# Feed-forward pieces between the taps of a deformable convolution, and rolling row buffers in place of padded images

## The chip, the cores and the metric

The kernel runs on one core of one Trainium2 chip. The metric is the device time of one execution in microseconds (us). The engines are called PE (TensorE), DVE (VectorE), ACT (ScalarE), POOL (GpSimd) and SP (SyncE); "PEld" is the weight load of PE. Each engine works through its own list of instructions in order and waits on semaphores that other engines or finished DMAs raise.

## The reference

The input is `x`, four images of 256 channels on a 64 x 64 grid, in float32. Everything is computed in float32.

```python
x = x + conv(ln_c(x))            # ln_c: layer norm over the channels of a pixel
t = tokens(x)                    # 4096 tokens of 256 channels per image
t = t + ffn(ln_t(t))             # ln_t: layer norm over the channels of a token
```

`conv` is three modulated deformable 3 x 3 convolutions, each followed by a relu. In each, an ordinary 3 x 3 convolution gives 27 numbers per pixel: for each of the 9 taps a row offset, a column offset and a mask. Tap k of a pixel reads the image at its shifted, fractional position (bilinear, zeros outside), times the sigmoid of the mask; the 9 x 256 samples of a pixel are then multiplied by a 2304 x 256 matrix.

`ffn` is a mixture of 8 experts. The softmax of 8 logits ranks the experts of a token, the best two are kept with their probabilities as weights, and each expert is `gelu(z @ W1 + b1) @ W2 + b2` with 512 hidden units.

## The kernel before, in words

A framework builds the program: the code names tiles out of pools with a fixed number of buffers, the framework adds the semaphore waits, and a list scheduler puts each engine's instructions into an order that need not be that of the code.

**Work units.** An image is cut into 8 blocks (`NB`) of 512 pixels, that is 8 rows. A stage is one convolution layer on one image; there are 12, ordered in pairs of images: (layer, image) = (0,0), (0,1), (1,0), (1,1), (2,0), (2,1), then the same for images 2 and 3. For each image the input of a layer lies in two places: as a zero-padded image in SBUF (`xpad`, read by the offset convolution) and as a table in DRAM (`tab`), whose row for a pixel holds 256 values and 256 differences to the pixel one row below, so that two neighbouring table rows (4 KB) are all that one sample needs.

**One block of the convolution** is `main_block`. For each tap k there are four groups of 128 pixels. For each group POOL issues an indirect DMA that gathers 128 x 4 KB from `tab` into `g` (L323, 8 buffers); DVE blends the two rows (L330); ACT scales the left column into `s` (L335); DVE adds the right column (L340); PE transposes `s` in two pieces (L345). ACT copies the transposed samples to `sT` (L352), and four 128 x 128 by 128 x 512 matmuls add them to `acc` (L355; the trace holds two records for each). After the ninth tap ACT applies the relu (L365). In layers 0 and 1 DVE copies the result into `xpad`, and PE, ACT and SP transpose it, copy it and store it in the table of the next layer (L377, L382, and `store_steps` with `dd`, L171, for the differences). In layer 2 the block is added to `x`, transposed and stored as tokens `t` (L374 to L387).

**One block of offsets** is `off_block`: 18 matmuls into `po` (L248), a small matmul into `pm` (L261), a sigmoid, and some 14 small DVE operations that give the gather indices `idx` and the blend factors `cf`. `main_block(i, n)` is followed by `off_block(i + 1, n)`, which belongs to the other image of the pair. **`pre_block`** normalises a block of `x` and writes the first table. It runs for images 0 and 1 ahead of all stages, and for images 2 and 3 beside the main blocks of the two layer-2 stages of the first pair.

**The feed-forward** begins when all 12 stages are done, with pools of its own. Per image: `prologue` loads a block of tokens, normalises it, and computes logits, softmax and ranks; `route` turns the choices into slots, sorted by expert, in tiles of 256 slots (39 tiles, `NF`); `dispatch` scatters the normalised tokens to those slots in `zs` in DRAM, by 64 indirect DMAs of 128 rows of 1 KB from POOL (L603); `expert` (39 times) loads the weights of a tile's expert by two indirect DMAs (L616, skipped inside the DMA if the expert is that of the tile before; one buffer), loads the tile from `zs` by SP, transposes it (`ftp`, L631), multiplies by W1 (`ph`, L642), applies gelu (L651), multiplies by W2 (`py`, L657), adds the bias on DVE (`y`, L665) and stores it in `ys`; `combine` gathers the two results of each token (`gy`, L681, 64 indirect DMAs per image), adds them to the token, transposes and stores. The prologue, route and dispatch of image b + 1 and the combine of image b - 1 are placed between the experts of image b.

Two consecutive scatters write the same DRAM tile `zs`, so each waits until the one before has landed.

## Time and profile before

| | |
|---|---|
| three runs | 8577.3, 8572.57, 8595.02 us (median 8577.3) |
| the profiled execution | 8566.52 us, its span 8564.6 us |
| first and last relu of a main block (L365) | at 314.8 and 6287.3 us of the span |
| busy PE, DVE, ACT, POOL | 6694.2, 5057.5, 3344.6, 4441.2 us |
| matmuls of the taps (L355) | 3353.7 us |
| indirect DMAs: gathers / weights / scatters / result gathers | 3456 / 312 / 256 / 256 |

The span falls into two parts: the convolutions up to about 6290 us, and the feed-forward of four images after it. A block of the convolution lasts from one relu group of L365 to the next. "Busy" of PE counts modelled ends of pipelined matmuls. In a wait, the instruction that waited stands before the arrow and what released it after it.

### The profile page before, as it was taken

The page shows a single profiled execution, that of the slowest core. Times are in us where ns is not written, and L with a number is a line of the kernel's source. Part 1 is how long each engine was busy: PE and PEld are TensorE (multiplying, and loading weights), DVE is VectorE, ACT ScalarE, POOL GpSimd, SP SyncE. Part 2 cuts the span into 40 slices and gives each one's busy share as a digit, 9 for nine tenths or more (in the row PEclk, how much of TensorE's full clock was granted, in tenths as well). Part 3 has the DMA queues.
Part 4 walks back from the last instruction along what each step waited for, and adds up shares of the span by engine and source line. Part 5 has one row for each costly group of instructions (what it writes and reads, how often), then busy time and mean ns, then how long its engine had stood idle before and what let it go on. Part 6 is the DMA issues. An engine that isn't in the chain of part 4 may idle for free.

```text
span 8564.6 us, 91686 instructions
## 1 busy us (share of the span) xinstructions
PE 6694.2 (78%) x26776; PEld 3737.0 (44%) x26776; DVE 5057.5 (59%) x11216; ACT 3344.6 (39%) x6860; POOL 4441.2 (52%) x4289
## 2 busy tenths in 40 slices
PE   7888888888888888888888888777753928658285
PEld 3444434444444444444344444343432827547274
DVE  4677767777677777777677777566662323323122
ACT  3454544444444444444444444344421212112011
POOL 0466556665555566566656656466623243433434
PEclk8999999999999999999999999899966969879697
DMA  5899989999899999999989999999942224333243
GB/s 163 278 329 328 329 314 324 335 321 331 316 321 321 315 324 334 328 326 328 324 309 333 322 333 331 358 331 333 335 146 79 87 99 133 113 102 123 82 128 121
DMA packets 791821, 2246.18 MB, mean 262 GB/s; under 512 B 131976, under 2 KB 245128, under 8 KB 789784
## 3 DMA queue, kind: packets, MB, share of 16 engines
q0 software_dynamic: 567168, 1917.26, 63.2%
q1 hardware_dynamic: 224152, 323.06, 11.4%
q8 instruction: 214, 3.51, 0.2%
q14 instruction: 287, 2.35, 0.1%
HBM read 2154.08 MB, written 232.31 MB: 279 GB/s over the span
## 4 chain that ended last, share of the span: by engine, by line
PE 50%; DMA 12%; DVE 12%; ACT 12%; issue 11%; POOL 2%; ACTq 0%; SPq 0%; POOLq 0%; DVEq 0%
PE acc L355 23%; ACT s L335 7%; PE tp L345 7%; PE po L248 6%; DVE g L330 6%; DMA zs<-z,slots 5%; PE ph L642 5%; PE py L657 4%; ACT sT L352 3%; DMA w<-in_W,wrow 3%; DVE s L340 2%; DMA g<-tab,idx 2%; DMA gy<-ys,slots 1%; PE tpo L377 1%; ACT r L365 1%
## 5 line engine op out<-in xcount | busy, mean ns | idle before, releaser
L323 POOL DMA_INDIRECT g<-tab,idx x3456 | 3628.6, 1050 | 2640.4 <-DVE s L340 1812.5
L355 PE MATMUL acc<-sT,wk 128*128 128x512 f32 x6912 | 3353.7, 630 | 347.3 <-ACT sT L352 345.6
L330 DVE SCALAR_TENSOR_TENSOR g<-g,cf 128x512 f32<-128x512 f32 x3456 | 2518.2, 745 | 94.1 <-DMA g<-tab,idx 93.5
L340 DVE SCALAR_TENSOR_TENSOR s<-g,cf,s 128x256 f32<-128x256 f32 x3456 | 1607.0, 483 | 1552.7 <-ACT s L335 1541.1
L335 ACT ACTIVATE s<-g,cf 128x256 f32<-128x256 f32 x3456 | 1682.1, 511 | 1925.6 <-DVE g L330 1886.6
L355 PEld LDWEIGHTS acc<-sT,wk 128*128 128x128 f32 x6912 | 1301.4, 198 | 2024.4 <-issue 1230.2
L345 PE MATMUL tp<-ident,s 128*128 128x128 f32 x6912 | 1024.5, 280 | 340.3 <-DVE s L340 302.7
L352 ACT COPY sT<-tp 128x512 f32<-128x512 f32 x1728 | 927.2, 590 | 865.0 <-PE tp L345 864.6
L345 PEld LDWEIGHTS tp<-ident,s 128*128 128x128 f32 x6912 | 811.2, 143 | 961.8 <-DVE s L340 453.0
L616 POOL DMA_INDIRECT w<-in_W,wrow x312 | 312.7, 1002 | 843.9 <-ACT hT L651 363.1
L248 PE MATMUL po<-xpad,wo 128*32 128x512 f32 x3456 | 719.4, 629 | 32.7 <-ACT xpad L220 20.8
L651 ACT ACTIVATE hT<-ph,w 128x256 f32<-128x256 f32 x624 | 258.8, 470 | 1143.9 <-PE ph L642 1143.5
L642 PE MATMUL ph<-fzT,w 128*128 128x256 f32 x2496 | 592.3, 392 | 65.7 <-DMA w<-in_W,wrow 65.2
L657 PE MATMUL py<-w,hT 128*128 128x256 f32 x2496 | 588.7, 390 | 54.8 <-DMA w<-in_W,wrow 44.9
L631 PE MATMUL ftp<-ident,zt 128*128 128x128 f32 x624 | 96.7, 283 | 613.7 <-DMA zt<-zs 604.2
L642 PEld LDWEIGHTS ph<-fzT,w 128*128 128x128 f32 x2496 | 481.5, 196 | 157.3 <-DMA w<-in_W,wrow 87.2
L657 PEld LDWEIGHTS py<-w,hT 128*128 128x128 f32 x2496 | 475.7, 196 | 131.5 <-issue 42.9
L603 POOL DMA_INDIRECT zs<-z,slots x256 | 251.6, 983 | 483.1 <-DMA zs<-z,slots 345.4
L665 DVE TENSOR_TENSOR y<-py,w 128x512 f32<-128x512 f32 x156 | 107.6, 690 | 466.4 <-PE py L657 466.4
L635 DVE COPY fzT<-ftp 128x512 f32<-128x512 f32 x156 | 107.3, 689 | 438.4 <-PE ph L642 317.7
L631 PEld LDWEIGHTS ftp<-ident,zt 128*128 128x128 f32 x624 | 76.7, 147 | 628.9 <-DMA zt<-zs 606.6
L681 POOL DMA_INDIRECT gy<-ys,slots x256 | 247.1, 965 | 147.5 <-issue 57.9
(136 smaller groups left out, 3073.2 us busy)
## 6 DMA issues: line engine op xcount, KB each, us to landing
g<-tab,idx POOLq DMA_INDIRECT x3456, 6.1
zt<-zs SPq DMA_DIRECT2D x156, 256.0 KB, 3.1
ys<-y SPq DMA_DIRECT2D x156, 256.0 KB, 2.0
tab<-h SPq DMA_DIRECT2D x128, 256.0 KB, 6.5
tab<-hd SPq DMA_DIRECT2D x128, 256.0 KB, 9.0
zs<-nil SPq DMA_DIRECT2D x12, 1664.0 KB, 25.6
xc_pre<-in_x SPq DMA_DIRECT2D x32, 512.0 KB, 4.5
tab<-h_pre SPq DMA_DIRECT2D x64, 256.0 KB, 3.3
```

What stands on the lines that cost most here:

```text
L248: nc.tensor.matmul(po[g * Q : (g + 1) * Q, :], lhsT=wo[:, k, c, :], rhs=xp[:, c, RPB * n + ky : RPB * n + ky + RPB, kx : kx + W], start=(m ...
L323: nc.gpsimd.indirect_dma_start(out=g, out_offset=None, in_=tb, in_offset=bass.IndirectOffsetOnAxis(ap=idx[:, n, j : j + 1], axis=0),)
L330: nc.vector.scalar_tensor_tensor(v[:, :, 0, :], v[:, :, 1, :], cf[:, n, j, 0:1], v[:, :, 0, :], ALU.mult, ALU.add,)
L335: nc.scalar.activation(s, v[:, 0, 0, :], AF.Copy, scale=cf[:, n, j, 1:2])
L340: nc.vector.scalar_tensor_tensor(ss[u], gs[u][:, 1, 0, :], cf[:, n, j, 2:3], ss[u], ALU.mult, ALU.add)
L345: nc.tensor.transpose(tp[:, c, (t0 + u) * P : (t0 + u + 1) * P], ss[u][:, c * P : (c + 1) * P], ident,)
L352: nc.scalar.copy(sT[:, c, :], tp[:, c, :])
L355: nc.tensor.matmul(acc[:, o, :], lhsT=wk[:, k, c, o * P : (o + 1) * P], rhs=sT[:, c, :], start=(k == 0 and c == 0), stop=(k == K - 1 and c ...
L616: nc.gpsimd.indirect_dma_start(out=w, out_offset=None, in_=ins[src], in_offset=bass.IndirectOffsetOnAxis(ap=st["wrow"][:, f : f + 1], axis=0),
L642: nc.tensor.matmul(ph[:, h, :], lhsT=w1[:, o : o + P], rhs=zT[:, c, :], start=(c == 0), stop=(c == CC - 1),)
L651: nc.scalar.activation(hT[:, h0 + h, :], ph[:, h, :], AF.Gelu, bias=w1[:, k : k + 1])
L657: nc.tensor.matmul(py[:, u, :], lhsT=hT[:, h, u * P : (u + 1) * P], rhs=w2[:, h * C : (h + 1) * C], start=(h == 0), stop=(h == HC - 1),)
```

## The change

The program is rewritten as one class, `Weave`, with one set of pools for the whole run.

- **Order of the stages.** (0,0), (1,0), (0,1), (2,0), (1,1), (0,2), (2,1), (1,2), (0,3), (2,2), (1,3), (2,3), so that an image is finished after stages 3, 6, 9 and 11 (counted from 0). Only image 0 is normalised ahead of the stages; `pre_block` of images 1, 2, 3 runs beside stages 0, 3 and 6, right after each main block.
- **Rolling row buffers.** `xpad` goes. Each block of a layer's output is written into a window of 10 rows (`win`, three buffers, four more ones in the first stage); ACT copies one row from and to the neighbouring window, DVE forms `dd` and a copy `vv`, PE transposes both (16 transposes, as before in number), ACT copies them to `hv`, SP stores whole 2 KB table rows. The offsets of block n - 1 of the same image's next layer are computed when block n is there (`rows_done`).
- **Tokens.** The main block of layer 2 ends with `tokens`: the sum with `x`, the normalisation, logits, softmax and ranks, which were `tpo`, `h` and `prologue`. Both `t` and the normalised `z` go to DRAM.
- **The queue.** When an image's last block is done, its `route`, 32 dispatch pieces of two scatters, 39 experts and 16 combine pieces of four result gathers go into a queue with a weight each. After each tap `pump` adds a rate to a credit and takes pieces whose weight it covers. The rate spreads an image's pieces over 2.9, 2.9 and 1.9 stages for images 0, 1, 2; image 3 has no stage after it, and its pieces come one after the other at the end.
- **Buffers.** `g` has 10 buffers in place of 8, `s` 5 in place of 6; expert weights have two buffers, and are skipped if the tile two before had the same expert; `ph` and `py` have one PSUM buffer each in place of two; all transposes share three PSUM banks in place of two buffers of two banks.
- **Engines.** The feed-forward's copies out of PSUM (`fzT`, `zT`, `o`) go from DVE to ACT; half of the relu goes from ACT to DVE; the sigmoid is written with tanh.

The core of the diff, whose new lines are shown with the functions that they call:

```diff
-    with ExitStack() as conv:
-        convolutions(conv, tc, ins, x, B, dram, t_dram, ident, eps_c)
-    with ExitStack() as ffn:
-        feed_forward(ffn, tc, ins, out_v, B, dram, t_dram, ident, eps_t)
+    Weave(ctx, tc, ins, out).run()
...
+    def rows_done(self, l, b, n, wins):
...
+        if n > 0:
+            nc.scalar.copy(w[:, :, 0, 1 : W + 1], wins[n - 1][:, :, RPB, 1 : W + 1])
+            nc.scalar.copy(wins[n - 1][:, :, RPB + 1, 1 : W + 1], w[:, :, 1, 1 : W + 1])
+        self.store_table(l, b, n, w)
+        if n > 0:
+            self.off_block(l, b, n - 1, wins[n - 1])
+        if n == NB - 1:
+            self.off_block(l, b, n, w)
...
+        for k in range(K):
+            sT = self.smT.tile([P, CC, BLK], F32, tag="sT", name=f"sT_{nm}_{k}")
+            for t0 in range(0, TPB, 2):
+                tp = self.ps.tile([P, CC, 2 * P], F32, tag="tp", name=f"tp_{nm}_{k}_{t0}")
...
+                nc.scalar.copy(sT[:, :, t0 * P : (t0 + 2) * P], tp)
...
+            if n == NB - 1 and i + 1 < len(self.stages):
+                self.load_tap(self.stages[i + 1][0], k, i + 1)
+            self.pump()
...
+        nc.scalar.activation(dst[0], src[0], AF.Relu, bias=bk[:, 0:1])
+        nc.vector.tensor_scalar(dst[1], src[1], bk[:, 1:2], 0.0, ALU.add, ALU.max)
+        if l < NL - 1:
+            self.rows_done(l + 1, b, n, wins)
+        else:
+            self.tokens(b, n, r)
...
+    def tokens(self, b, n, r):
...
+        nc.sync.dma_start(self.t_dram[b][n], tok)
+        normalise(nc, self.small, tok, z, self.eps_t, nm)
+        nc.sync.dma_start(self.z_dram[b][n], z)
...
+        if n == grp.n1 - 1:
+            self.enqueue(grp)
...
+    def dispatch(self, grp, n, t):
+        m = n * TPB + t
+        for i in range(2):
+            self.nc.gpsimd.indirect_dma_start(
+                out=self.zs[grp.i % 2],
+                out_offset=bass.IndirectOffsetOnAxis(ap=grp.slots[:, i, m : m + 1], axis=0),
+                in_=grp.z[:, t, :],
+                in_offset=None,
+            )
...
+    def expert(self, grp, f):
...
+        if f == 0:
+            self.weights(grp, 0)
+        if f + 1 < grp.NF:
+            self.weights(grp, f + 1)
+        w1, w2 = self.w1[f % 2], self.w2[f % 2]
...
+            ph = self.ps1.tile([P, 2, FT], F32, tag="ph", name=f"ph_{nm}_{h0}")
...
+    def enqueue(self, grp):
+
+        nb = grp.n1 - grp.n0
+        q = [(2.0, lambda: self.route(grp)), (20.0, lambda: None)]
+        for n in range(nb):
+            q.append((0.0, lambda n=n: self.dispatch_load(grp, n)))
+            for t in range(TPB):
+                q.append((2.0, lambda n=n, t=t: self.dispatch(grp, n, t)))
+        q.append((15.0, lambda: None))
+        for f in range(grp.NF):
+            q.append((8.0, lambda f=f: self.expert(grp, f)))
+        q.append((15.0, lambda: None))
+        for n in range(nb):
+            q.append((0.0, lambda n=n: self.combine_load(grp, n)))
+            for t0 in range(0, TPB, 2):
+                q.append((4.0, lambda n=n, t0=t0: self.combine(grp, n, t0)))
+        taps = grp.stages * NB * K
+        rate = sum(w for w, _ in q) / taps if taps else 0.0
+        self.queue += [(w, rate, fn) for w, fn in q]
+
+    def pump(self):
+        if not self.queue:
+            self.credit = 0.0
+            return
+        self.credit += self.queue[0][1]
+        while self.queue and self.queue[0][0] <= self.credit:
+            w, _, fn = self.queue.pop(0)
+            self.credit -= w
+            fn()
+
+    def run(self):
+
+        self.stages = [
+            (0, 0), (1, 0), (0, 1), (2, 0), (1, 1), (0, 2),
+            (2, 1), (1, 2), (0, 3), (2, 2), (1, 3), (2, 3),
+        ]
+
+        beside = {0: 1, 3: 2, 6: 3}
+
+        self.groups = [Group(b, 0, NB) for b in range(self.B)]
+        for i, (g, s) in enumerate(zip(self.groups, (2.9, 2.9, 1.9, 0))):
+            g.i, g.stages = i, s
...
+        for i in range(len(self.stages)):
+            wins, pre = {}, {}
+            for n in range(NB):
+                self.main_block(i, n, wins)
+                if i in beside:
+                    self.pre_block(beside[i], n, pre, i == 0)
+        while self.queue:
+            self.queue.pop(0)[2]()
```

## The prediction

> **What bounds the kernel now.** I read the busy table by slices first, then windows of single stretches, then the timeline of one tap. The slices:
>
> ```profile
> PE   7888888888888888888888888777753928658285
> POOL 0466556665555566566656656466623243433434
> PEclk8999999999999999999999999899966969879697
> DMA  5899989999899999999989999999942224333243
> ```
>
> Two parts are to be seen: 28 slices in which PE is 80 to 90% busy and the DMA engines over 90%, and 11 in which neither is. The windows give numbers (a stretch of convolution; the first image's scatters; its experts; a dense part of those):
>
> ```profile
> core 0: us, PE busy (x) PEld busy (x) DVE busy (x) ACT busy (x) POOL busy (x), PEclk, DMA share, GB/s
> 1000.00:6170.00 5170.00, 4363.26 (x16281) 2122.60 (x16280) 3648.97 (x7308) 2471.15 (x5090) 3095.43 (x2946) 0.95 0.92 327
> 6388.00:6566.00 178.00, 0.00 (x0) 0.00 (x0) 25.48 (x100) 2.08 (x7) 65.01 (x66) 0.50 0.22 75
> 6566.00:6900.00 334.00, 308.14 (x1545) 263.85 (x1546) 111.66 (x399) 87.83 (x177) 86.77 (x88) 0.99 0.29 93
> 6600.00:6800.00 200.00, 187.03 (x957) 160.84 (x956) 63.37 (x229) 54.23 (x110) 44.48 (x45) 0.99 0.27 89
> ```
>
> The scatters leave PE idle for 178 us; the experts run PE at 93.5%. The scatters in the timeline:
>
> ```profile
> 6421.35 0.97 POOL L603 DMA_INDIRECT zs<-z,slots  x1 [1.71 <-DMA zs<-z,slots]
> 6424.03 0.97 POOL L603 DMA_INDIRECT zs<-z,slots  x1 [1.70 <-DMA zs<-z,slots]
> ```
>
> Each waits for the one before to land: 2.68 us apart. Inside the convolution, a tap where nothing else is interleaved:
>
> ```profile
> 1196.45 3.70 PE L355 MATMUL acc<-sT,wk 128*128 128x512 f32 x8 [0.73 <-ACT sT L352]
> ...
> 1201.70 0.44 PE L345 MATMUL tp<-ident,s 128*128 128x128 f32 x2 [0.90 <-DVE s L340]
> 1202.87 3.70 PE L355 MATMUL acc<-sT,wk 128*128 128x512 f32 x8 [0.73 <-ACT sT L352]
> ```
>
> A tap takes 6.42 us here, and PE waits in it for DVE's samples and for ACT's copy. PE's own work per tap is (3353.7 + 1024.5) / 864 = 5.07 us, from the rows
>
> ```profile
> L355 PE MATMUL acc<-sT,wk 128*128 128x512 f32 x6912 | 3353.7, 630 | 347.3 <-ACT sT L352 345.6
> L345 PE MATMUL tp<-ident,s 128*128 128x128 f32 x6912 | 1024.5, 280 | 340.3 <-DVE s L340 302.7
> ```
>
> Blocks, from relu to relu (a plain one, then one with a normalised block beside it):
>
> ```profile
> 4428.41 1.26 ACT L365 ACTIVATE r<-acc,bk 128x512 f32<-128x512 f32 x2 [0.78 <-PE acc L355]
> 4489.65 1.26 ACT L365 ACTIVATE r<-acc,bk 128x512 f32<-128x512 f32 x2 [0.78 <-PE acc L355]
> ```
> ```profile
> 2695.91 1.26 ACT L365 ACTIVATE r<-acc,bk 128x512 f32<-128x512 f32 x2 [0.78 <-PE acc L355]
> 2760.33 1.26 ACT L365 ACTIVATE r<-acc,bk 128x512 f32<-128x512 f32 x2 [0.59 <-PE acc L355]
> ```
>
> Over the timeline plain blocks take 60 us, those in the two stages with `pre_block` 67; the one change of stage that waits for a table just written costs 94 - 60 = 34. PE is busy about 54 of the 60. So the convolution is bound by PE plus latency between DVE, ACT and PE; the feed-forward, 2277 us after the last relu, by experts on PE and by scatters and gathers one by one.
>
> **The change part by part.** The sum follows the new order; the old one stands at 6287 us at its last relu.
>
> *Start.* Eight normalised blocks go ahead in place of sixteen. In the opening stretch one starts about every 17.5 us together with its offsets: 140, then 85 for gather landing and the first main block, its end included: 225 at the first relu (before: 314.8; bounds 205 and 250).
>
> *Stage 0*, seven further blocks, with a normalised block and a second set of offsets beside each: 67 plus 18 offset matmuls and the small ones, (719.4 + 98.8) / 96 = 8.5: 75 each, 525 (bounds 67, all hidden, and 90, all in series).
>
> *Two stage changes* need the table just written, (0,0) to (1,0) and (1,3) to (2,3): 68. Other changes of stage keep a stage in between.
>
> *Plain blocks*, 7 stages x 8. The transposes are the same in number; DVE gains the copy `vv` (priced by two `xpad` copies, 0.88) and half the relu (0.69, as a copy of this size out of PSUM) and loses the two copies; the chain relu, row copies, `dd`, `vv` is some 2 us longer, and six offset matmuls (2.5 us) now stand in it. I take 60, 3360 (bounds 58 and 63; the three shared PSUM banks argue for the upper one).
>
> *Token blocks with a normalised block* (stages 3 and 6, 16 blocks). PE's list has the token transposes, then transposes of `z`, then logits, then the normalised block, one behind the other, so PE waits through add 1.2, copies 1.2, four statistics 2.3, square root with its table load 1.6, normalising 1.6, copies 1.2, and about 0.2 per hand-over, with a few blends between: 17 us over today's 67. 84 each, 1344. Below: today's prologue took 98 us for eight blocks, pipelined, 12 each: 79. Above: 96, if rank and softmax, 4 us of DVE, and the second table load also stand in the chain, and more blends fall in it.
>
> *Token blocks alone* (stages 9, 11; 16 blocks). No offsets and no table, but without offsets the last stage has 59.5 today, so that gives nothing; the logits come some 8 us later than today's transposes, minus what DVE blends ahead: 66, 1056 (bounds 60 and 75).
>
> Convolution: 225 + 525 + 68 + 3360 + 1344 + 1056 = 6578.
>
> *Experts of images 0 to 2*, 117. Each has (96.7 + 592.3 + 588.7) / 156 = 8.19 us of PE. Fully in PE's idle 6 us per block (2.65 experts a block) each would cost 5.9; at the PE share of the dense window, (54 + 21.7) / 0.935 = 81 per block, 7.9. The scheduled order has taps' transposes between `ph` and `py`, so ACT's gelu is covered. I take 7.5: 878 (upper bound 9.0, with a wait for the single `ph` buffer).
>
> *Scatters.* They now stand in POOL's list with one or two gathers after each. Three POOL issues take 3 x 1.24 (0.94 and 0.30 idle in the timeline) = 3.7 us; an idle machine lands a scatter in 2.4. I take 3.9 from scatter to scatter: 64 x 3.9 = 250 us of POOL, in which 27 taps of 6.67 (18 for image 2) would have passed: 70 + 70 + 130, a little of it caught up at block ends: 240. Gathers queued behind a waiting scatter are `g` tiles for DVE, and ten buffers cover two and a half taps. Below: 3.4, if the next issue never waits, 145. Above: landing as the median gather in the convolution, 6.1, plus issue, 7.1: 850.
>
> The page "DMA: Bandwidth & Descriptors" of the Trainium skill (Queues, rings and completion order; Latency and other measured facts) speaks against the change here: an engine consumes its ring in order, and access to the DRAM takes 0.2 us on average, 2 at high load. By that a scatter in the convolution lands some 1.8 us later than the 2.4 of the trace, an estimate of about 4.5 between scatters and 115 more in the sum, 8548; no row of the trace has a scatter under load.
>
> *Result gathers.* 64 x 1.24 = 80 us of POOL per image, against a spare 60 - 36 x 1.24 = 15 us per block over three blocks (two for image 2): 35 + 35 + 50 = 120 (below 40, if `combine` finds POOL idle).
>
> *Cover.* Some 18 experts fall into token blocks, where PE idles: they cost 3.5 there, -70.
>
> *Tail, image 3.* Tokens 25, route 10, 64 x 2.68 = 172, landing and loading 6, 39 experts at 9.0 (8.36 by the dense window's 200 us, plus the single `ph`) = 351, combine as today's last, 110: 674 (bounds 640 and 710). Double weight buffers remove the waits of `ph` and `py` for weights (110 us in all today); the gelu wait is late next. The DMA bytes that the second buffer adds, 3 x 8 loads of 128 x (1028 + 1280) x 4 bytes or 28 MB, lie beside PE work, since stretched taps need fewer gathers per us than the 327 GB/s.
>
> Span 6578 + 878 + 240 + 120 - 70 + 674 = 8420, with 2 us around it 8422, against 8566.5 of the profiled execution, which lies 0.13% below the median of 8577.3. On the median's scale: **8433 us**, 1.7% less.
>
> **The rivals.**
> (1) *Scatters land late*, and POOL's list holds up the gathers: slower. For it: 92% DMA share and 6.1 us to land a gather. Against it: only two gathers ahead of each scatter. It costs 192 us per us of period over 3.9, and decides at 3.9 + 144 / 192 = 4.65; at 5.5, 8740.
> (2) *Token chains are longer*: 32 blocks. It decides at 4.5 us more per block; at 96 and 75, 8770. For it: DVE has some 65 us of work in the longer kind (36 x 1.23 for samples, 9 for tokens, 5 for normalising, 4 for offsets, 3 for the table). Against it: blended rows wait ready, so taps after it run at 5.1.
> (3) *The pieces don't hide*: a block's matmuls wait at each piece for DVE and ACT to refill; 11 us per expert gives 8845. The scheduled order, which mixes them finely, speaks against it.
> (4) *PE fills up*: 6734 us of PE work (6694 plus 256 transposes), less 350 in the tail, at 90%: 7090, and 674: about 7780; half way, 8080. For it: PE waits in taps that have DVE time to spare. Against it: scatters and chains give PE nothing to do.
>
> **How the numbers follow.** Forecast 0.42 (8300 to 8540), rival 4 0.12, a shortfall that ends near today 0.06, rival 1 0.20, rival 2 0.14, rival 3 0.06. Faster by over 0.3% (about what a measurement of this kernel can tell from no change): 0.42 + 0.12 = 0.54; within 0.06; slower 0.40. The likeliest case's own range is 8300 to 8540; the range for 8 in 10 takes in half of rival 4 and most of 1 and 2: 8100 to 8860.
>
> **What the profile after would show.** Right: relus 60 us apart in stages 1, 2 and 10, about 80 with experts, 84 in stages 3 and 6; scatters at 3.9; the last relu near 7750, and about 670 after it. Wrong: scatters apart by over 4.65 with DVE waiting for `g`; token blocks over 90; PE waiting for `s` right after each `py`.

## The result, and the profile after

The changed kernel takes 8633.36 us (median of four runs, 8624.77 to 8641.94), the kernel before 8577.05: a ratio of 1.0062, 95% interval 1.0043 to 1.0081. It is slower by 0.6%, inside the range of 8100 to 8860, on the other side of no change than forecast.

Times below are compared within one set of runs measured together, because in some sets the kernel before itself took 8680 to 8703 us, and the changed kernel 8902 where it ran beside it (ratio 1.0249, 1.0202 to 1.0296), with ACT standing still for reasons that the trace doesn't name (last section).

The slices of the page of after (busy tenths in 40 slices of the span of 8640.1 us), to be set against those of before:

```profile
PE   5788888877776899988777799998776698777096
PEclk8999999998888999998888899998888899888597
DMA  5887999987777888876787888887797787768233
```

PE is no longer busy in one long stretch and idle in another. Its row rises and falls with the stages: 9 where experts lie between plain blocks (slices 15 to 17 and 24 to 27), 7 in the stages with tokens (9 to 12, 20 to 22). The first image's scatters pull it down in slice 13. DMA falls to 7 in the token stages too, so a full DMA is not what holds them. Windows of single stretches give the numbers. The columns are the window, its length, then busy time (and instructions) of each engine, the granted clock of PE, the DMA share and GB/s. The windows are the opening gathers and first block, plain blocks, eight blocks with tokens and a normalised block, four blocks with scatters, eight plain blocks with experts, and the last image's scatters:

```profile
core 0: us, PE busy (x) PEld busy (x) DVE busy (x) ACT busy (x) POOL busy (x), PEclk, DMA share, GB/s
160.00:268.00 108.00, 59.49 (x157) 26.52 (x152) 50.87 (x104) 31.12 (x61) 45.66 (x47) 0.78 0.99 396
881.00:1376.00 495.00, 419.75 (x1635) 204.04 (x1634) 355.74 (x731) 238.45 (x504) 304.33 (x288) 0.98 0.92 327
1871.50:2576.60 705.10, 518.69 (x2022) 275.30 (x2022) 466.06 (x1124) 314.01 (x615) 323.59 (x287) 0.84 0.70 253
2576.60:2926.00 349.40, 246.88 (x796) 112.41 (x796) 185.29 (x348) 123.44 (x249) 222.37 (x212) 0.86 0.81 270
3229.50:3844.90 615.40, 569.24 (x2423) 341.30 (x2421) 377.89 (x755) 272.46 (x613) 340.44 (x333) 0.99 0.86 302
7998.50:8220.00 221.50, 11.23 (x45) 9.03 (x46) 16.77 (x58) 6.91 (x11) 66.34 (x68) 0.51 0.22 75
```

Only the stretch with experts between plain blocks does what the change is written for: PE is busy for 569.24 of 615.40 us, 92.5%, nearly as in the dense experts of before (93.5%). In the token stage it is 518.69 of 705.10, 74%, and the clock granted to it is 0.84. In the scatter stretch it is 71%.

Three groups of the page of after (busy time, mean ns, idle time before and what ended it) show what is new among the waits, and a fourth line is the row of before that belongs to the second:

```profile
L467 PE MATMUL acc<-sT,wk 128*128 128x512 f32 x6912 | 3393.7, 635 | 216.8 <-ACT sT L464 212.7
L445 DVE SCALAR_TENSOR_TENSOR g<-g,cf 128x512 f32<-128x512 f32 x3456 | 2546.9, 747 | 1384.1 <-DMA g<-tab,idx 1369.3
L664 POOL DMA_INDIRECT zs<-zl,slots x256 | 266.1, 1040 | 399.9 <-DMA zs<-zl,slots 311.3
```
```profile
L330 DVE SCALAR_TENSOR_TENSOR g<-g,cf 128x512 f32<-128x512 f32 x3456 | 2518.2, 745 | 94.1 <-DMA g<-tab,idx 93.5
```

DVE waits 1369 us for gathers, against 93.5 before. That looks like the reason for the loss; an experiment below takes the weight loads out of POOL's list and finds that they are not what the wait or the time comes from. POOL waits 311 us for scatters to land, 116 of it after the last relu.

**Where the time went.** Block by block, from relu to relu of L486 (a stage is counted from its first relu to the first of the next, so that its last block holds the change of stage):

| | prediction | after |
|---|---|---|
| first relu | 225 | 268.4 |
| stage 0, first seven blocks | 525 | 521.2 |
| the two stage changes that wait for a table | 68 | about 32 (91.9 - 75 and 103.4 - 88) |
| plain blocks without pieces (stages 1, 2) | 60.0 | 61.9 on average; 61.6, the last of a stage 66 |
| token blocks with a normalised block (stage 3) | 84 | 88.1 on average; 84.6 to 88.4, the last 101.7 |
| last relu | 7746 | 7998.5 |
| after it | 674 | 641.6 |

So everything that is missing was lost ahead of the last relu (7998.5 - 7746 = 252 us); the end was 32 us shorter than forecast (642 for 674).

### The profile page after: what moved, and what is told of

It is laid out like the page before. It is cut to its first block, busy times and chain, and to the rows that moved or that the text cites. A ratio compares the mean times of both kernels' runs of the same rounds, so it can differ in the third digit from the quotient of the medians.

```text
span 8640.1 us, 92087 instructions
## 1 busy us (share of the span) xinstructions
PE 6778.1 (78%) x27032; PEld 3829.6 (44%) x27032; DVE 4998.0 (58%) x10768; ACT 3516.7 (41%) x7349; POOL 4492.8 (52%) x4289
## 5 line engine op out<-in xcount | busy, mean ns | idle before, releaser
L467 PE MATMUL acc<-sT,wk 128*128 128x512 f32 x6912 | 3393.7, 635 | 216.8 <-ACT sT L464 212.7
L450 ACT ACTIVATE s<-g,cf 128x256 f32<-128x256 f32 x3456 | 1625.8, 510 | 1878.8 <-DVE g L445 1192.4
L455 DVE SCALAR_TENSOR_TENSOR s<-g,cf,s 128x256 f32<-128x256 f32 x3456 | 1577.2, 481 | 912.7 <-ACT s L450 906.4
L459 PE MATMUL tp<-ident,s 128*128 128x128 f32 x6912 | 1078.3, 284 | 515.9 <-DVE s L455 499.6
L464 ACT COPY sT<-tp 128x512 f32<-128x512 f32 x1728 | 961.0, 585 | 887.4 <-PE tp L459 882.0
L731 PE MATMUL py<-w,hT 128*128 128x256 f32 x2496 | 637.4, 388 | 23.0 <-ACT hT L726 20.2
L319 PE MATMUL po<-win,wo 128*32 128x512 f32 x2304 | 410.7, 611 | 102.2 <-ACT win L255 95.1
L664 POOL DMA_INDIRECT zs<-zl,slots x256 | 266.1, 1040 | 399.9 <-DMA zs<-zl,slots 311.3
L319 PE MATMUL po<-win_pre,wo 128*32 128x512 f32 x1152 | 240.2, 713 | 37.5 <-ACT win_pre L255 18.4
L289 ACT COPY hv<-tpv 128x512 f32<-128x512 f32 x384 | 198.3, 599 | 165.0 <-PE tpv L284 163.3
```

The source lines that it names most:

```text
L319: nc.tensor.matmul(po[g * Q : (g + 1) * Q, :], lhsT=self.wo[l][:, k, c, :], rhs=w[:, c, ky : ky + RPB, kx : kx + W], start=(m < NQ), stop= ...
L450: nc.scalar.activation(s, g[:, 0, 0, :], AF.Copy, scale=cf[:, j, 1:2])
L455: nc.vector.scalar_tensor_tensor(ss[u], gs[u][:, 1, 0, :], cf[:, j, 2:3], ss[u], ALU.mult, ALU.add)
L459: nc.tensor.transpose(tp[:, c, u * P : (u + 1) * P], ss[u][:, c * P : (c + 1) * P], self.ident,)
L464: nc.scalar.copy(sT[:, :, t0 * P : (t0 + 2) * P], tp)
L467: nc.tensor.matmul(acc[:, o, :], lhsT=self.wk[k][:, c, o * P : (o + 1) * P], rhs=sT[:, c, :], start=(k == 0 and c == 0), stop=(k == K - 1 ...
```

## The experiments

**The convolution part and the pieces told apart.** `pump` returns at once, so all pieces come after the last stage; each image's `route` runs when the image is finished.

```diff
-        q = [(2.0, lambda: self.route(grp)), (20.0, lambda: None)]
+        self.route(grp)
+        q = []
...
     def pump(self):
+        return
```

> The changed kernel with every feed-forward piece held back until the last convolution block is done (only the routing of an image is computed when the image is finished). It separates the price of the new convolution part (rolling rows, token chains, start) from the price of the pieces that go between the taps. Theory A (the convolution part without pieces is longer than the old one by its token chains, and the pieces then still gain a lot by going between the taps): plain blocks stay at 61.6 us, blocks with tokens and a normalised block at 86, blocks with tokens alone at about 75 with PE idle for some 20 us of each; the last relu near 6870 us, four feed-forwards of about 610 us behind it, 9330 us in all, so that going between the taps is worth about 700 us. Theory B (the pieces cost as much between the taps as they cost alone, and the convolution part is as short as the old one): token-alone blocks at 62 to 64 us, last relu below 6600, total within 2% of the 8633 us.

It took 9375.49 us, 1.0797 (1.0748 to 1.0847) of the kernel before, but ACT's stalls without a releaser came to 1500 us there, and the changed kernel was not beside it. A second run in another set gave 1.0928 (1.0899 to 1.0956) with the same stalls; a third had the changed kernel beside it:

> The changed kernel as the base of the three beside it. Two kinds of measurement have been seen: one in which the kernel before takes 8577 to 8600 us and ACT has under 200 us of idle time without a named releaser, and one in which it takes 8680 to 8703 and kernels derived from the changed one have 900 to 1500 us of such time. In the first kind the ratio is 1.005 again; in the second, if the disturbance reaches the changed kernel more than the one before, 1.02 to 1.035.

> Every piece held back until the last convolution block is done, once more beside the changed kernel, to subtract like from like. Theory A: undisturbed, the last relu comes near 6870 us, and the pieces between the taps cost about 1120 us in the changed kernel (predicted 1168); disturbed, 7120 to 7220 against 8250 to 8300 in the changed kernel, 1100 as well. So the step that failed is the convolution part, which the prediction had at 6578. Theory B: less than 6700 undisturbed, and the pieces cost over 1300.

The changed kernel took 8901.92 us in this set, the kernel with all pieces at the end 9361.36, 1.0780 (1.0716 to 1.0843) of the kernel before. The last relu in each (ACT's instruction, its duration, its start), first with the pieces at the end, then in the changed kernel of the same set:

```profile
L486 ACT ACTIVATE r<-acc,bk x1: 687/687/687, 7091.1 to 7091.1; 128x512 f32<-128x512 f32 x1
```
```profile
L486 ACT ACTIVATE r<-acc,bk x1: 687/687/687, 8259.2 to 8259.2; 128x512 f32<-128x512 f32 x1
```

The difference is 1168 us. The scheduler had lifted the first image's 64 scatters into stages 3 and 6 of the kernel with the pieces at the end, where the second of these stages is 35 us longer than the first; with that, the pieces of three images cost about 1200 us between the taps. The prediction had 878 + 240 + 120 - 70 = 1168. Taken from the first measurement's 7998.5, this leaves about 6800 us for the convolution part alone. Both runs of the subtraction hold the stalls, at about the same rate (ACT's waits without a releaser up to the last relu add up to 821 us of 8259 and 648 of 7091), so 1200 is somewhat too much. Added up stage by stage in the first measurement, which has few such waits, the pieces cost 1146 us (against 495 for a plain stage, 705 for one with tokens and a normalised block, 72 for a block with tokens alone, 16 for the stage change in stage 10), which leaves 6852. So the convolution part takes 6800 to 6850 us, where the prediction had 6578, and the pieces 1150 to 1200. Theory A holds: the pieces were priced right as a sum, the convolution part was not.

It also shows what going between the taps is worth. At the end the four feed-forwards take 9364.9 - 7091.1 = 2274 us, 568 each, as in the kernel before (2277). Three of them cost 1150 to 1200 between the taps in place of 1700. The changed kernel still loses. Its convolution part is 510 to 560 us longer than the old one (6800 to 6850 against 6287; the new one holds the work of tokens and logits, which stood in the feed-forward before), and its feed-forward only 440 to 490 shorter (the pieces and the 642 at the end, against 2277).

**The chains at block ends.** In a token block, the timeline of PE in the changed kernel (start, duration, instruction, idle time before it and what ended it) shows one stop after another:

```profile
1962.87 1.94 PE L517 MATMUL tp_tok<-ident,r 128*128 128x128 f32 x8 [4.91 <-DVE r L509]
1969.55 1.09 PE L530 MATMUL ztp_tok<-ident,z_tok 128*128 128x128 f32 x4 [4.75 <-DVE z_tok L64]
1971.32 1.88 PE L540 MATMUL lp_tok<-gw,zT_tok 128*128 128x8 f32 x8 [0.68 <-ACT zT_tok L536]
...
1982.34 0.66 PE L404 MATMUL tp_pre<-ident,h_pre 128*128 128x128 f32 x2 [4.70 <-DVE h_pre L64]
```

`late_both` moves two of these chains. The transposes of `z`, logits and ranks of a block are computed after the second tap of the next block, and `pre_block` in two halves after the fourth and sixth tap of the main block, in place of behind it.

```diff
             if n == NB - 1 and i + 1 < len(self.stages):
                 self.load_tap(self.stages[i + 1][0], k, i + 1)
+            if hook and k == KP:
+                hook = hook()
+            if hook and k == KP + 2:
+                hook()
+            if k == KL and self.later:
+                self.later()
+                self.later = None
             self.pump()
...
         nc.sync.dma_start(self.z_dram[b][n], z)
+        self.later = lambda: self.rank(b, n, grp, nm, z, lg)
```

> The changed kernel itself once more, as the base of the three kernels that run beside it. In the four runs before this one engines stood still for reasons that their traces don't name (1000 to 1500 us of ACT's idle time has no releaser, against 95 in the kernel before and 167 in the changed kernel), and the kernel before took 1.2% longer than in the first measurement. If this is the chip, the changed kernel shows it too, and its ratio to the kernel before is up to 1.03; on a chip like the first one it is again 1.004 to 1.008.

> The changed kernel with two chains moved away from the ends of blocks: the transposes of the normalised tokens, the logits and the ranks of a block are computed after the second tap of the next block, and the normalised block of the next image in two halves after the fourth and the sixth tap of the main block in place of behind it. Nothing else changes. Theory A (in the token stages PE stands idle for some 20 us of every block because these chains stand one behind the other in its list): blocks with both go from 86 to about 72 us, blocks with tokens alone from 75 to about 65, the first stage's from 75 to 72: 16 x 14 + 16 x 9 + 8 x 3 = 390 us less than the changed kernel beside it, a ratio to that of 0.955 (0.945 to 0.975). Theory B (these blocks are long by the work of DVE and PE that they hold, the order does not matter): less than 100 us, 0.99 or more.

In this set the changed kernel took 8635.08 us, 1.0047 (1.0031 to 1.0063) of the kernel before, as in the first measurement. `late_both` took 8303.82, 0.9661 (0.9644 to 0.9679) of the kernel before: 331 us, or 3.8%, less than the changed kernel. Blocks of stage 3 take 70 to 76 us in place of 85 to 88. By stage, changed kernel and `late_both`: stage 3 705 and 583, stage 6 780 and 690, stage 9 662 and 617, the first seven blocks of stage 11 651 and 608, stage 0 615 and 581; the other stages agree within 20 us each. The first relu comes 28 us later, since both halves of a `pre_block` now stand inside the first main block. Stage 3 in its window (columns as above), and PE in the same place of a block of it:

```profile
1871.40:2454.40 583.00, 474.08 (x1972) 260.63 (x1972) 447.75 (x1107) 297.10 (x604) 310.57 (x287) 0.92 0.86 305
```
```profile
2022.95 1.94 PE L534 MATMUL tp_tok<-ident,r 128*128 128x128 f32 x8 [5.27 <-DVE r L526]
...
2033.03 0.56 PE L551 MATMUL ztp_tok<-ident,z_tok 128*128 128x128 f32 x3 [1.53 <-DVE z_tok L66]
2033.42 3.60 PE L475 MATMUL acc<-sT,wk 128*128 128x512 f32 x8
```

The wait of 4.75 us ahead of the transposes of `z` is 1.53 here, because taps stand in front of it. Over the stage, PE's groups with the two moved chains (busy time, mean ns, idle time before), first in the changed kernel and then in `late_both`:

```profile
L530 PE MATMUL ztp_tok<-ident,z_tok 128*128 128x128 f32 x64 | 17.4, 428 | 41.9 <-DVE z_tok L64 41.9
L404 PE MATMUL tp_pre<-ident,h_pre 128*128 128x128 f32 x64 | 16.8, 380 | 37.5 <-DVE h_pre L64 32.5 <-DVE w_tok L584 5.0
```
```profile
L551 PE MATMUL ztp_tok<-ident,z_tok 128*128 128x128 f32 x64 | 10.8, 285 | 6.7 <-DVE z_tok L66 6.7
L412 PE MATMUL tp_pre<-ident,h_pre 128*128 128x128 f32 x56 | 9.7, 285 | 3.2 <-ACT sT L472 1.8 <-DVE h_pre L66 1.5
```

Some 70 us of waits are gone; the wait ahead of the tokens' own transposes, which were not moved, stays (46.6 us, then 46.8). PE's busy share of the stage rises from 74 to 81%. Theory A holds with a gain of 331 for 390. This is the largest single cause that an experiment shows: of the 210 us that stage 3 takes over a plain stage (705 against 495), 122 come from the order of two chains, and the other 88 stay with the work itself and the chain that was not moved.

**Scatters that don't wait for each other.** The second choices go to a tensor of their own, which no expert reads.

```diff
-                out=self.zs[grp.i % 2],
+                out=(self.zs, self.zo)[i][grp.i % 2],
```

> The changed kernel in which the scatters of the second choices go to another DRAM tensor than those of the first choices, so that a scatter waits for the landing of the one two before it instead of the one before it. Left out of the computation: the experts see empty slots in place of the second choices; the number and the size of all instructions stay. Theory A (in the scatter blocks the waits of POOL's list for the landing hold up the gathers): the 12 scatter blocks fall from about 88 us to about 75 (36 x 1.24 + 18 x 1.29 = 68 us of issue is what remains on POOL), the 64 scatters after the last block take about 90 us in place of 172, the one block of 150 us also goes back to 90 because the last scatter then stands further ahead of the first expert in the lists: together some 130 + 80 + 55, about 8370 us (8300 to 8450). Theory B (the number of POOL issues, not the wait, stretches these blocks): scatter blocks stay above 84 us and only the part after the last relu gets shorter, 8500 us or more.

It took 8769.48 us, 1.0089 (1.0061 to 1.0116) of the kernel before; `fill_late` and `gap` of the same set stand at 1.0223 and 1.0306. POOL's waits ahead of scatters are 311.3 us in the changed kernel, in 193 waits (row of L664 above). In this one, for the half of the scatters that write `zs` (waits in us, and how many):

```profile
  DMA zs<-zl,slots: 41.4, 40
```

After the last relu 559 us are left in place of 643, as expected (84 us). Inside the stages the gain is small: stage 4 takes 656 us against 681 and 686 in those two, stage 7 647 against 671 and 663. That is some 23 us per image, where 130 were expected for three. Neither theory fits as it stands, and B comes nearer: the waits went, but the scheduler then put up to 22 scatters into a block (32 in one), and 36 gathers and 22 scatters at 1.27 us of POOL each are 74 us, longer than a plain block (these blocks took 80 to 93). So the landing is about a quarter of the hundred us that an image's scatters cost between gathers. That the rest is their place in POOL's list is likely from this count, but no run shows it alone.

**Scatters spread thinner.**

```diff
-                q.append((2.0, lambda n=n, t=t: self.dispatch(grp, n, t)))
+                q.append((5.0, lambda n=n, t=t: self.dispatch(grp, n, t)))
```

> The changed kernel with a weight of 5 in place of 2 for each piece of two scatters, so that about 10 scatters fall into a block over six blocks in place of 18 over three and a half; the experts stand a little closer for it. In the lists the first expert of the third image stands 18 gathers behind its last scatter, in place of 15 ahead. Theory A (POOL has some 15 us to spare per block, and 18 scatters with their waits need 44): scatter blocks go from 88 to 66 to 70 us, the 64 scatters of an image cost 40 us in place of 100, the block of 150 us is gone: 150 to 200 us less than the changed kernel beside it, ratio 0.977 to 0.983. Theory B (each scatter costs what it costs, 1.5 us, wherever it stands): within 0.5% of the changed kernel, but for the 55 us of the one block.

8637.02 us, the changed kernel beside it 8635.08: nothing. Yet the scatter blocks did shrink. Six of them:

```profile
2591.80:3026.70 434.90, 333.10 (x1204) 155.81 (x1204) 269.73 (x529) 184.06 (x374) 291.34 (x276) 0.94 0.86 299
```

That is 72.5 us a block with 10 scatters. Against plain blocks of 61.6 the first image's 64 scatters cost 70 us in place of 99, and the block of 150 us is 85. Stages 4, 7 and 10 together are 183 us shorter. But the seven experts per image that stood in stage 4 or 7 now stand further on: stages 5, 6, 8, 9 and 11 are 174 us longer together. An expert costs 5.5 us where 2.7 of them fall into a plain block, 6.4 where 3.1 do ((654.6 - 495) / 25), and 6 to 10 in the token stages. The total is that of theory B, but for another reason: the scatters did get cheaper, as theory A has it. The pieces of an image have a fixed number of taps to lie in, and what was won at one end of them was lost at the other.

**The block that stood still.** In the changed kernel 150.6 us pass between the third and the fourth relu of stage 10. One row of PE's timeline tells why:

```profile
6834.74 1.09 PE L705 MATMUL ftp<-ident,zt 128*128 128x128 f32 x4 [54.64 <-DMA zt<-zs]
```

The first expert of the third image stands in PE's list ahead of taps whose gathers stand in POOL's list ahead of the last scatters; it needs all scatters, so PE stops until POOL has worked through its list with the buffers it has. `gap` raises the credit between the last scatter and the first expert.

```diff
-        q.append((15.0, lambda: None))
+        q.append((15.0 if grp.i != 2 else 75.0, lambda: None))
         for f in range(grp.NF):
```

> The changed kernel in which, for the third image alone, the credit to be saved between the last scatter and the first expert is 75 in place of 15. In the lists the first expert's transposes then stand behind the last scatter's place by 17 gathers, as for the first two images (18), in place of ahead of it by 15. Theory A (PE waits at that expert for all scatters, while the gathers that the scatters stand behind wait for PE to free their buffers' successors): the third block of the eleventh stage falls from 150 to about 90 us, the experts that start later are pushed into the last stage at about 6 us each, total 8575 to 8600 us. Theory B (that block is long by its 21 scatters and its first experts themselves): it stays above 120 us and the total within 15 us of 8633.

The block takes 85.7 us, so the mechanism is right, as theory A has it, but the total does not gain: 8945.94, 1.0306 (1.0276 to 1.0336) of the kernel before, with `fill_late` at 1.0223 in the same set. From stage 10 to the last relu it takes 769 + 702 us, `fill_late`, which keeps the stall, 773 + 668. The higher weight raises the rate at which the later pieces come (four to five experts a block in place of four), and by these stage times they cost what the stall had cost.

**The zero-filling stores.**

```diff
-        for z in self.zs:
-            r = 0
-            while r < nf * FT:
...
+                if 3 <= i < 6:
+                    self.fill_some()
                 self.main_block(i, n, wins)
```

> The changed kernel with the 40 zero-filling stores of the slot buffers (20 MB) moved from the start into the stages from the fourth on, three ahead of each main block. Theory A (the first gathers share the DMA engines with that fill, 419 GB/s for about 47 us): the first relu falls from 268 to about 225 us, the blocks that now hold the fill grow by 0 to 15 us in all, total 8590 to 8605 us. Theory B (the first block is late because its gathers start all at once and its tap weights load, whatever else is stored): the first relu stays above 258 us and the total within 10 us of 8633.

The first relu comes at 238.7 us, in the three others of the set at 268.5 to 269.2; the total is 8865.41, 1.0223 (1.0187 to 1.0259) of the kernel before. The stages that now hold the fill (3 and 4) are 4 to 5 us longer together than in `gap` (734 + 681 against 725 + 686). So 30 us of the 43 that the start lost belong to the fill: theory A, with less than it forecast. What the total gains is not shown, since the changed kernel did not run in this set. DMA issues of the changed kernel between 160 and 268 us (bytes of the queue in MB and its share; KB of each issue, and the median us to landing for the gathers):

```profile
q1 hardware_dynamic: 6135, 20.87, 48.8%
...
zs<-nil SPq DMA_DIRECT2D x37, 512.0 KB
g<-tab,idx POOLq DMA_INDIRECT x47, 18.6
```

Half of what the DMA engines did while the first block waited for its gathers was storing zeros, and a gather took 18.6 us to land.

The kernel before pays for the same fill, in another place. The first two relus of its stage 10, (2, 2), at 5353.7 and 5447.5 us, stand 94 us apart. Its 12 zero-filling stores of 1664 KB, 20 MB, are issued between 5340 and 5376 us, and between those two relus a gather takes 11.1 us to land, where the median of the run is 6.1. DMA issues of the kernel before between the two relus:

```profile
zs<-nil SPq DMA_DIRECT2D x9, 1664.0 KB, 33.5
g<-tab,idx POOLq DMA_INDIRECT x34, 11.1
```

No other block of the kernel before is over 81 us, so this is the 94 that the prediction took for a change of stage that waits for a table just written. But the table that stage 10 reads was written in stage 8. So the old profile already held the price of the fill, 94 - 60 = 34 us, under another name; this is read from the trace, no run moves the fill there.

**Does DVE's waiting for gathers cost anything?** 304 of the 312 weight loads are left out of POOL's list.

```diff
-        if f + 1 < grp.NF:
-            self.weights(grp, f + 1)
+        if f == 0:
+            self.weights(grp, 1)
```

> Left out: 304 of the 312 indirect weight loads, so most experts use another expert's weights; this time beside the changed kernel. Theory A (DVE's 1369 us of waiting for gathers is slack, because PE is busy in the blocks with experts): 0 to 60 us less than the changed kernel beside it. Theory B (the weight loads in POOL's list hold the taps up): 150 us less or more.

It took 8937.73 us, 1.0280 (1.0227 to 1.0334), the changed kernel beside it 8901.92, 1.0249: no gain. (An earlier run without the changed kernel beside it gave 1.041.) DVE's wait, without the loads and then with them:

```profile
L445 DVE SCALAR_TENSOR_TENSOR g<-g,cf 128x512 f32<-128x512 f32 x3456 | 2546.5, 748 | 1432.8 <-DMA g<-tab,idx 1344.3 <-issue 70.1 <-PE po L319 4.7
```
```profile
L445 DVE SCALAR_TENSOR_TENSOR g<-g,cf 128x512 f32<-128x512 f32 x3456 | 2543.2, 747 | 1324.8 <-DMA g<-tab,idx 1232.0 <-issue 78.1 <-DVE g L445 3.0
```

The loads neither cause the wait nor cost time, which leaves theory A. In the expert blocks PE is the engine that is full (92.5% in stage 5), so an engine ahead of it can wait without loss there.

**Versions meant to beat both.** `combo` joins the late chains, the thin scatters and the late fill. `best` leaves the scatters as they were and lowers the third image's rate, so that its last 23 experts run among the last image's scatters, and its result gathers among the last image's experts.

```diff
-        for i, (g, s) in enumerate(zip(self.groups, (2.9, 2.9, 1.9, 0))):
+        for i, (g, s) in enumerate(zip(self.groups, (2.9, 2.9, 4.2, 0))):
...
+        for part, beside in ((new[:2], []), (new[2:s], ex), (new[s:e], cb), (new[e:], [])):
+            done = 0
+            for m, q in enumerate(part):
+                q[2]()
+                while done < len(beside) * (m + 1) // len(part):
+                    beside[done][2]()
+                    done += 1
```

> The two changes of order of the runs beside it together (late chains, thin scatters), and the zero-filling stores moved out of the start as before (30 us). Theory A: the gains add, 390 + 170 + 30 = 590 us less than the changed kernel, a ratio to it of 0.93 and of 0.94 to the kernel before. Theory B (once one wait is gone another engine sets the same block times): less than half of that, not below 0.97 of the changed kernel.

> The late chains of late_both, the zero-filling stores out of the start, and another sharing of the third image's pieces: a lower rate, so that 16 of its 39 experts run between taps of the last two stages, and 23 experts stand between the scatters of the last image, where PE idled for 172 us, its result gathers between the experts of the last image, where POOL idled. Theory A (what an expert costs is decided by where it stands: nothing beside scatters without convolution, 6 to 8 us in the last two stages): from the 8304 us of late_both, 54 us for the start, 60 us for the block that stood still, 23 x 6.5 + 50 us for pieces taken out of the last stages, and 40 us back for a longer tail: about 8040 us (7980 to 8150), ratio to the kernel before 0.937. Theory B (the scatters and the weight loads of those experts wait for each other in POOL's list): the tail grows by 150 us or more, total above 8150.

> The kernel of best again beside the changed kernel. In its first run the part after the last relu took 731 us in place of 642, and the parts before it were longer by the stalls without a releaser. Theory A: with undisturbed engines 8100 to 8200 us, a ratio of 0.945 to 0.955 to the changed kernel and 0.945 to 0.96 to the one before; with disturbed ones 0.95 to the changed kernel too. Theory B (the experts between scatters give back what the stages gain): no better than late_both, 0.962 of the changed kernel.

`combo`: 8287.26 us, 0.9632 (0.9616 to 0.9648), only 17 us under `late_both`, although its first relu comes 55 us earlier. The gains don't add: of the 590 us of theory A, 348 came, 331 of them with the late chains alone. That is theory B in kind, though at 0.960 of the changed kernel it lies below B's bound of 0.97. `best`: 8508.49, 0.9767 (0.9746 to 0.9788) in one set, and 8394.40, 0.9656 (0.9608 to 0.9705) in another, where the changed kernel stands at 1.0249: by the medians 0.943 of the changed kernel, where `late_both` is 0.962 of it in its set. That is theory A of the last expectation; the 8040 us of the one before were not reached. All three versions beat both kernels. Whether `best` beats `late_both` without the stalls was not measured. The part after its last relu in two windows, the first of which holds most of the scatters:

```profile
7674.40:7900.00 225.60, 181.85 (x770) 144.85 (x771) 29.99 (x78) 51.64 (x112) 96.05 (x95) 0.89 0.45 141
7900.00:8399.00 499.00, 372.35 (x1628) 293.89 (x1626) 89.02 (x171) 106.94 (x240) 211.25 (x217) 0.86 0.48 150
```

PE is busy for 81% of a stretch in which it did 11 us of work in 221. The end grows from 642 to 725 us for 23 more experts and 64 more result gathers, at most 3.6 for each expert, where the expectation had them at 6 to 8 in the last stages.

## Why the prediction was right or wrong

**Wrong: the convolution part, 6578 us, where 6800 to 6850 was needed.** This is the step that turned a forecast gain of 1.7% into a loss of 0.6%. By its own terms:

- *Start, 225 (bounds 205 and 250): 268.4*, outside the bounds. The eight normalised blocks, at 17 us each as forecast, were done at 162 us in place of 140: the step left out the 24 us before PE's first instruction. The 85 us for gathers and the first block became 106, because 20 MB of zeros are stored just there; with the fill moved they are 77. The step looked at the engines of the opening and not at what the SP queue sends beside it. +43.
- *Plain blocks, 60 (58 to 63): 61.9*, with the change of stage in it, and 1.9 x 56 = 106. The 60 was the row of a block inside a stage. Whole stages of the kernel before, counted from first relu to first relu, give 61.9 as well: its eight stages of layers 0 and 1 without a normalised block beside them took 495.3 us on average, for 495.0 in stages 1 and 2 now. Inside a stage the blocks did grow, from a median of 60.4 to 61.6, and the block with the change of stage shrank, from 63 to 81 to 66. So of the 15 us that such a stage is over the forecast, about half is that growth, and the rest is what the row of 60 left out. Whether the longer chain of row copies, `dd`, `vv` and offsets made the growth is not shown.
- *Token blocks with a normalised block, 84: 88.1* on average in stage 3 (+33; stage 6, which also holds pieces, is taken to be like it). *Token blocks alone, 66 (60 to 75): 73 to 74* in the third run with pieces at the end, where plain blocks are 2 to 3% longer than elsewhere; some 72, or +90 for 15 blocks. The argument that blends lie ready did hold (six taps after the chain, from 1998.75 to 2028.23 us, take 4.5 to 5.7 us each), but it was counted in full against a chain that stops PE three times for 4.7 to 4.9 us, in a stage with a granted clock of 0.84. `late_both` shows that 122 us of stage 3, 15 a block, are the order of these chains: most of the 21 that such a block takes over the 67 of the kernel before.
- *Stage 0* was right (521 for 525). The *stage changes* were dearer in the forecast (68 for 32): its 34 each was the block with the zero fill in the kernel before, read as a stage change. By luck this covers most of the 43 that the start lost.

These make 43 + 106 + 66 + 90 - 4 - 36 = 265, so 6843. This is rival 2, just past its mark (66 + 90 over 31 blocks are 5.0 us a block, where it was to decide at 4.5), and beside it the start and the plain blocks, which no rival named. The error lies on one side in nearly every term: each value with bounds was taken below their middle.

**Right as a sum by luck, wrong in its parts: the pieces, 1168 us, measured at 1150 to 1200.** Experts in plain stages cost some 156 us less than forecast (87 at 5.7 in place of 7.5), scatters some 90 more, and what stands in token stages some 45 more. Against plain stages of 495 us:

- *Experts at 7.5: 5.5 and 5.9* in stages 5 and 8 ((615.5 - 495) / 21.75 and (625.8 - 495) / 22), below the row that the step took for it; the lower value of 5.9, which counts on PE's idle time in a block, was the better one.
- *Scatters, 240 us: about 330.* With 5.7 us for each expert beside them: 100 in stage 4, 93 in stage 7, 137 in stage 10 (less 16 for its stage change), the last with the 55 us in which PE stood at the third image's first expert, a cost that was not foreseen at all. The period was forecast at 3.9 and is 4.9 (88 us for 18): three issues of POOL as forecast, and a wait of 1.0 us for the landing ((311.3 - 115.6) / 192) on top. Rival 1 was to decide at 4.65, so it came true in part. An excerpt of POOL's timeline:

```profile
2659.82 1.02 POOL L664 DMA_INDIRECT zs<-zl,slots  x1 [4.01 <-DMA zs<-zl,slots]
2661.14 1.40 POOL L439 DMA_INDIRECT g<-tab,idx  x1 [0.30 <-issue]
2662.85 1.12 POOL L439 DMA_INDIRECT g<-tab,idx  x1 [0.31 <-DVE s L455]
2664.28 0.99 POOL L664 DMA_INDIRECT zs<-zl,slots  x1 [0.30 <-issue]
...
2670.76 1.00 POOL L664 DMA_INDIRECT zs<-zl,slots  x1 [2.81 <-DMA zs<-zl,slots]
```

  The scatter issued at 2664.28 holds up the next until 2670.76, 6.5 us, where 2.68 stood between scatters with nothing beside them. The 63 scatters of that stretch (2576 to 2926 us) take a median of 4.2 us to land, where the page of before has 2.4:

```profile
DMA to landing us min/median/max: 2.5/4.2/7.4
```

  The estimate that the prediction worked out from the Trainium skill ("DMA: Bandwidth & Descriptors", Queues, rings and completion order; Latency and other measured facts) had 1.8 us more for the landing and 4.5 between scatters. The first is what this case shows, and the second is nearer to 4.9 than the 3.9 that the prediction took.
- *Cover, -70: none that large.* Token stages cost 72 us (stage 6 against stage 3), 91 and 156 us (9 and 11, against 72 a block) more than without pieces, for 30 experts and 192 result gathers. If the gathers cost the forecast's 120, an expert costs 6.6 there, not 3.5. The likely reason is that PE, idle in a chain of its own list, cannot take up an expert that stands behind the chain; no run shows it alone.

**Right:** the tail in kind and nearly in size (674 forecast, 642 measured), most scatters of the last image at 2.68, experts on a full PE between plain blocks.

The signs that the text named for being wrong did show: scatters more than 4.65 apart, with DVE waiting for `g`; token blocks near 90 (88 on average in stage 3). The last relu came at 7998, not 7750.

## What to carry to other kernels

Work put between other work is worth only what the engine's list leaves free where it lands: fill stretches in which PE stands idle because of POOL (experts among scatters: at most 3.6 us each), not those that already run PE at 90% or stop it with a chain of their own. When a block's end grows a chain (normalise, transpose, project), move its later links behind the next taps before moving anything else; that alone gave 331 us here. In a forecast, read a term with a factor of 56 from whole stages, their changes included, and sum terms that all lean one way once at their other end. And before giving one odd block a cause, look at what every queue sends in it: the 94 us block of the kernel before held the zero fill that the forecast of the start left out.

## What the runs showed of the hardware

**The granted clock of PE is lower in stretches where PE stops more.** It is 0.99 and 0.98 in the stages with PE 92.5 and 85% busy, 0.92 at 81%, 0.84 and 0.86 at 74 and 71%, 0.78 at 55% in the opening and 0.51 at 5% (windows above); 0.84 and 0.86 stand in the other order, so the share alone does not set it. The same kinds of instruction take longer in the token stage of the changed kernel (granted clock 0.84) than in `late_both` (0.92). Logits and offsets of stage 3 by groups (mean ns after the busy time), in the changed kernel and then in `late_both`:

```profile
L319 PE MATMUL po<-win_pre,wo 128*32 128x512 f32 x288 | 63.8, 723 | 8.7 <-ACT om L328 5.4 <-ACT win_pre L255 2.6 <-ACT win_pre L409 0.7
...
L540 PE MATMUL lp_tok<-gw,zT_tok 128*128 128x8 f32 x128 | 30.1, 364 | 10.8 <-ACT zT_tok L536 10.8
```
```profile
L322 PE MATMUL po<-win_pre,wo 128*32 128x512 f32 x270 | 43.1, 600 | 3.9 <-ACT om L331 3.9
...
L561 PE MATMUL lp_tok<-gw,zT_tok 128*128 128x8 f32 x128 | 16.6, 256 | 6.8 <-ACT zT_tok L557 6.8
```

364 against 256 ns for a logit matmul, 723 against 600 for an offset one. Of the 122 us that the stage lost with the chains moved, some 70 are the waits themselves, and some 45 are PE's busy time (518.69 - 474.08; the second has 50 recorded instructions fewer, 1972 for 2022, which is some 12 of the 45). So a chain that stops PE is paid twice here: in the stop, and in slower instructions around it.

**The same two kernels were 0.5 to 0.6% apart in two sets and 2.5% in another.** ACT's longest waits in the changed kernel of the set with 1.0249 (waits in us, how many, the longest), then in the first measurement:

```profile
ACT hT L726 <- issue: 249.1, 77, 4.4
ACT s L450 <- issue: 173.5, 148, 5.2
ACT sT L464 <- remote: 165.3, 66, 9.5
```
```profile
ACT hT L726 <- issue: 144.1, 37, 4.4
ACT s L450 <- issue: 20.6, 18, 1.6
```

In the first, ACT's waits with no named releaser ("issue" and "remote") add up to about 1030 us, in the second to 167. Kernel text and data are the same. What stops ACT was not found, nor why the changed kernel suffers more than the kernel before; a difference of 1% between such kernels has to be measured in one set.
